# Attention in four passes: the last two products of a pass are held back until the next pass has given out its first scores

## The chip, the cores and the metric

The kernel runs on one core of a Trainium2 chip. The metric is the device time of one execution in microseconds, as a median of several. An execution carries four layers; the change is in the last one.

## The reference, cut to what matters

The input is two images of 128 channels and 64 x 64 places. Four layers follow each other, each adding to its input a result computed from the group-normalized input. Layer 3, with `S` = 4096 places, 8 heads of 16 channels each:

```python
xf = x.reshape(B, C, S)
def proj(wt, bt):
    y = jnp.einsum('oc,bcs->bos', wt, xf) + bt[None, :, None]
    return y.reshape(B, Hh, Dh, S)
q, k, v = proj(wq, bq), proj(wk, bk), proj(wv, bv)
a = jnp.einsum('bhcq,bhck->bhqk', q, k) / jnp.sqrt(jnp.float32(C))
a = jax.nn.softmax(a, axis=-1)
o = jnp.einsum('bhqk,bhck->bhcq', a, v)
return o.reshape(B, C, h, w)
```

and then `x = x + layer3(groupnorm(x))`. So for each image and head there are 4096 x 4096 scores, an exponential of each, and a product with the values.

## The kernel before, in words

Layer 3 (`_layer3`) works in four passes: image 0 with heads 0 to 3, image 0 with heads 4 to 7, and the same for image 1. In a pass four heads lie side by side in the 128 partitions, 32 to each.

Inside a pass, `attend` goes over 8 blocks of 512 queries (`qb`) and in each over 32 tiles of 128 keys (`kt`). Such a step has three parts:

- `scores(qb, kt)`: eight matmuls on TensorE (L2094), two for each of the four heads, into two score tiles in PSUM (`ps_s`; the pool has three such tiles of two banks each). Then ScalarE takes the exponential of each tile (L2104) into two weight tiles in SBUF (`weights`; the pool has eight).
- `multiply(qb, kt, w)`: the product of weights and values (L2113), four matmuls in the source and eight in the profile[...]. They add up over all 32 key tiles in one of two PSUM accumulators (`ps_acc`).
- after the last key tile of a block, `done(qb, ps)`: VectorE copies the accumulator out (L2135), brings the sums to the places of the values (L2137), takes the reciprocal (L2138), multiplies (L2139) and adds the residual (L2140); the result goes out by DMA (L2142).

The order of the instructions on each engine is the order of the program: `_in_order` fixes it. TensorE is therefore kept from waiting for ScalarE by hand: scores are given out two steps ahead of their product. The list `waiting` holds the steps whose product is still to come. After the scores of a step, if more than two steps wait, the product of the oldest is given out. At the end of a pass the two that are left are given out one after the other (L2153 and L2154).

Other work is woven in. `work` is a generator that makes what a pass needs: the folded weights of an image (`folded`), the values (`values`, L2048 and L2055), queries and keys (`queries_and_keys`, L2022 to L2040), and after a pass has begun a bound on its scores (`bound`, L2068 to L2083). While one pass runs, the loop at the end of `_layer3` takes three steps of that generator in each block of queries, so that the next pass finds its queries, keys and values ready. In the first pass part of its own values and keys is made in this way too (`early`).

Of the kernel before, what the change touches and what calls it, by code (L numbers as in the profile page):

```python
# [1954 lines left out]
def _layer3(ctx, tc, X, l3, cst, out, worst, here):  # L1955
# [10 lines left out]
    def acc():  # L1966
        return accp.tile([128, CH], F32, tag="acc", name="ps_acc")
# [118 lines left out]
    def attend(b, t, q, k, vt, early):  # L2086
        ac = [None]

        def scores(qb, kt):
            ps = [spp.tile([128, 2, CH], F32, tag="sp", name="ps_s") for _ in range(2)]  # L2090
            for n in range(2):
                for j in range(4):
                    rows = slice(32 * j, 32 * j + 32)
                    nc.tensor.matmul(  # L2094
                        ps[j // 2][:, j % 2, :],
                        k[rows, kt * 128 : (kt + 1) * 128],
                        q[n][rows, qb * CH : (qb + 1) * CH],
                        start=(n == 0),
                        stop=(n == 1),
                    )  # L2100
            w = []
            for p in range(2):
                w.append(pp.tile([128, 2, CH], F32, tag="weights", name="weights"))
                nc.scalar.activation(w[p], ps[p], AF.Exp)  # L2104
            return w

        def multiply(qb, kt, w):
            if kt == 0:
                ac[0] = acc()
            for j in range(4):  # L2110

                i = j % 2
                nc.tensor.matmul(  # L2113
                    ac[0][32 * j : 32 * j + 32, :],
                    vt[:, kt, j // 2, i : i + 2, :].rearrange("p a d -> p (a d)"),
                    w[j // 2][:, i, :],
                    start=(kt == 0),
                    stop=(kt == NQT - 1),
                )
            if kt == NQT - 1:  # L2120
                done(qb, ac[0])

        def done(qb, ps):
            cols = slice(qb * CH, (qb + 1) * CH)

            places = [
                (slice(32 * j + 16 * (j % 2), 32 * j + 16 * (j % 2) + 16),
                 slice(64 * t + 16 * j, 64 * t + 16 * j + 16))
                for j in range(4)
            ]  # L2130
            xs = residual[qb % 2]
            for to, rows in places:
                nc.sync.dma_start(xs[to, :], X[rows, b, cols])
            u = two.tile([128, CH], F32, tag="u", name="u", bufs=1)
            nc.vector.tensor_copy(u, ps)  # L2135
            r = two.tile([128, CH], F32, tag="r", name="r", bufs=1)
            nc.vector.stream_shuffle(r, u, [(i + 16) % 32 for i in range(32)])  # L2137
            nc.vector.reciprocal(r, r)  # L2138
            nc.vector.tensor_mul(u, u, r)  # L2139
            nc.vector.tensor_add(u, u, xs)  # L2140
            for at, rows in places:
                nc.sync.dma_start(out[b, rows, cols], u[at, :])  # L2142

        waiting = []
        for qb in range(NCH):
            for kt in range(NQT):
                if kt % 2 == 0:
                    over = next(early, early) is early
                waiting.append((qb, kt, scores(qb, kt)))
                if len(waiting) > 2:  # L2150
                    multiply(*waiting.pop(0))
                yield kt if over else None
        for x in waiting:  # L2153
            multiply(*x)  # L2154

    def in_turn(*gens):
        gens = list(gens)
# [7 lines left out]
    def work():  # L2165

        for b in range(B):
            f = []
            yield from folded(b, f)
            for t in range(2):  # L2170
                first = b == 0 and t == 0
                q = [two.tile([128, S], F32R, tag=f"q{n}", name=f"q{n}") for n in range(2)]
                k = two.tile([128, S], F32R, tag="k", name="k")
                vt = two.tile([128, NQT, 2, 3, 16], F32, tag="vt", name="vt")
                early = values(b, t, f, vt)
                keys = queries_and_keys(b, t, f, q, k, 2 * first)
                if first:

                    for _ in range(2):
                        next(keys)  # L2180
                        next(early)
                        yield
                    early = in_turn(keys, early)
                else:
                    for _ in early:
                        yield
                    yield from keys
                yield b, t, (q, k, vt, early)
                yield from bound(b, t, q, k)

    def up_to_next(side):
        for x in side:
            if x:
                found.append(x)
                return
            yield

    side = work()
    found = []
    for _ in up_to_next(side):  # L2200
        pass
    while found:
        b, t, got = found.pop()
        beside = up_to_next(side)
        for kt in attend(b, t, *got):

            if kt in (4, 12, 20):
                next(beside, None)
        for _ in beside:
            pass  # L2210


def _input(nc, X, a, b):
# [31 lines left out]
def kernel(ctx, tc, a, out):  # L2245
# [4 lines left out]
    with tc.tile_pool(name="keep", bufs=1) as keep:  # L2250
# [5 lines left out]
        with tc.tile_pool(name="late", bufs=1) as late:  # L2256
            with tc.tile_pool(name="raw", bufs=1) as raw:
                with tc.tile_pool(name="l1_in", bufs=1) as l1_in:
                    consts = _layer1_inputs(nc, l1_in, a)
                    l3 = _layer3_inputs(nc, late, raw, a, a["consts2"])  # L2260
                    _layer1(tc, X, a, cst, st[:, :B], st[:, B], consts)
                _layer2(
                    tc,
                    X,
                    rows_of_weights,
                    cst,
                    a["consts1"],
                    st[:, B],
                    st[:, B + 1],
                    lambda: _layer3_weights(nc, l3),  # L2270
                )
            _layer3(tc, X, l3, cst, out, worst, st[:, B + 1])
# [69 lines left out]
```

## Time and profile before

| | us |
|---|---|
| executions timed | 4249.1, 4260.06, 4260.55 (median 4260.06) |
| profiled execution | 4252.46, span of the trace 4250.7 |
| TensorE busy (PE) | 4058.6, 95% of the span |
| ScalarE busy (ACT) | 3342.0, 79% |
| VectorE busy (DVE) | 2187.2, 51% |
| DMA, mean | 37 GB/s |
| layer 3 starts at about | 2275 |
| its passes end at about | 2780, 3274, 3764, 4236 |

How to read it: shares are averages over four layers with different limits, so they say little about a single stage. In layer 3 TensorE and ScalarE are both busy in nine tenths or more of nearly every slice, VectorE in one to three tenths. A piece "x8" in a timeline is eight instructions of one kind without a break; the time in front is its start, the next one its length, and what stands in brackets is how long the engine stood idle before it and what ended that. Matmuls overlap, so the lengths of pieces add up to more than the time that passes; the distance between starts doesn't have that fault.

### The profile page before, as it was taken

To read this page: it belongs to the slowest core of one execution; us is meant where nothing else is said; L and a number is where in the kernel's file an instruction comes from. 1 tells how busy PE (TensorE), PEld (TensorE's weight loads), DVE (VectorE), ACT (ScalarE), POOL (GpSimd) and SP (SyncE) were. 2 spreads that over 40 slices of the span, in tenths; PEclk is the share of its full clock that TensorE was granted. 3 is DMA by queue.
4 is the path that set the end of the run, shared out by engine and by line. 5 is a ranking of instruction groups with operands and counts; after the bars stand their busy time and mean duration, and the time that the engine had idled before them with its cause. 6 is when DMAs were issued, how large, how long until landed. Compare 5 with 4: busy or idle time off the path is not lost. (4 is left out here: it accounts for less than half of the span.)

```text
span 4250.7 us, 82260 instructions
## 1 busy us (share of the span) xinstructions
PE 4058.6 (95%) x35790; PEld 1552.1 (37%) x35790; DVE 2187.2 (51%) x2358; ACT 3342.0 (79%) x4051; POOL 70.4 (2%) x145
## 2 busy tenths in 40 slices
PE   7899999978999998997998999999999999999998
PEld 4523222245222223445665333333333333333332
DVE  3679999746999998986765211321032012211111
ACT  4478888734888884335655999999999999999998
POOL 1001000000000001000000000000000000000000
PEclk9999999999999999998999999999999999999999
DMA  1099970000000000003660000000000000000000
GB/s 48 2 194 191 182 89 1 1 1 2 1 1 1 1 1 12 1 1 128 270 263 4 6 6 4 6 6 4 6 6 6 4 6 6 6 4 6 6 6 4
DMA packets 158822, 158.86 MB, mean 37 GB/s; under 512 B 24809, under 2 KB 148713, under 8 KB 154354
## 3 DMA queue, kind: packets, MB, share of 16 engines
q1 hardware_dynamic: 158450, 153.50, 15.5%
q8 instruction: 282, 4.62, 0.4%
q14 instruction: 90, 0.74, 0.1%
HBM read 145.09 MB, written 73.40 MB: 51 GB/s over the span
## 5 line engine op out<-in xcount | busy, mean ns | idle before, releaser
L2104 ACT ACTIVATE weights<-ps_s 128x1024 f32<-128x1024 f32 x2048 | 1885.2, 1103 | 65.9 <-PE ps_s L2094 65.4
L1350 ACT ACTIVATE weights<-ps_s 128x1024 f32<-128x1024 f32 x1024 | 992.6, 1022 | 175.5 <-PE ps_s L1341 150.6
L2113 PE MATMUL ps_acc<-weights,vt 128*32 128x512 f32 x8192 | 1095.6, 607 | 0.0
L2094 PE MATMUL ps_s<-q,k 32*128 32x512 f32 x8192 | 925.9, 445 | 5.3 <-ACT weights L2104 5.3
L1792 DVE TENSOR_TENSOR sums<-sums,weights 128x2048 f32<-128x2048 f32 x384 | 879.1, 2289 | 42.2 <-ACT weights L1350 6.6
L2094 PEld LDWEIGHTS ps_s<-q,k 32*128 32x128 f32 x8192 | 472.6, 183 | 841.9 <-ACT weights L2104 775.2
L1341 PE MATMUL ps_s<-q,k 32*128 32x512 f32 x4096 | 647.4, 642 | 3.7 <-ACT weights L1350 1.3
L2135 DVE COPY u<-ps_acc 128x512 f32<-128x512 f32 x32 | 22.1, 692 | 1041.5 <-PE ps_acc L2113 1041.5
L1757 PE MATMUL ps_acc<-weights,vt 128*32 128x512 f32 x4096 | 548.8, 605 | 3.4 <-ACT used L1782 3.2
L1341 PEld LDWEIGHTS ps_s<-q,k 32*128 32x128 f32 x4096 | 210.4, 183 | 429.7 <-issue 209.9
L2113 PEld LDWEIGHTS ps_acc<-weights,vt 128*32 128x32 f32 x8192 | 163.2, 108 | 378.8 <-issue 366.8
L1757 PEld LDWEIGHTS ps_acc<-weights,vt 128*32 128x32 f32 x4096 | 81.0, 108 | 395.1 <-issue 377.0
L662 DVE SCALAR_TENSOR_TENSOR X<-g,w,X 128x2048 f32<-128x2048 f32 x84 | 197.4, 2351 | 2.6
L1792 DVE TENSOR_TENSOR sums<-weights 128x2048 f32<-128x2048 f32 x64 | 146.6, 2290 | 63.1 <-ACT weights L1350 63.1
L1546 PE MATMUL ps_sp<-pad,diag 32*32 32x512 f32 x4608 | 165.3, 600 | 4.6 <-DVE q L1564 3.1
L1008 PE MATMUL ps_z<-w_ri,e 128*32 128x128 f32 x2048 | 137.5, 409 | 14.4 <-DVE e L950 12.2
L2055 DVE TENSOR_TENSOR vt<-ps_acc,bv 128x384 f32<-128x384 f32 x32 | 17.8, 557 | 247.1 <-PE ps_acc L2048 247.1
L1524 PE MATMUL ps_sp<-xn,w_qkv 128*128 128x512 f32 x160 | 91.3, 709 | 33.5 <-DVE k L1564 16.0
L1546 PEld LDWEIGHTS ps_sp<-pad,diag 32*32 32x32 f32 x4608 | 95.1, 103 | 62.6 <-issue 15.4
L2025 DVE LOAD_MASK_SELECT qq<-ps_acc x32 | 0.4, 14 | 222.2 <-PE ps_acc L2022 222.2
L2138 DVE RECIPROCAL r<-r 128x512 f32<-128x512 f32 x32 | 107.3, 3353 | 1.1
L950 DVE TENSOR_SCALAR e<-ps_pe 32x136 f32<-32x136 f32 (+1 forms) x352 | 104.4, 297 | 5.0
(288 smaller groups left out, 2602.6 us busy)
## 6 DMA issues: line engine op xcount, KB each, us to landing
w_ri<-w_r SPq DMA_DIRECT2D x16, 2112.0 KB, 8.2
w_ri<-w_i SPq DMA_DIRECT2D x16, 2112.0 KB, 13.5
w_r<-in_L_conv_kr_w SPq DMA_DIRECT2D x15, 528.0 KB, 12.5
w_r<-in_L_conv_kr_x SPq DMA_DIRECT2D x15, 528.0 KB, 12.2
w_r<-in_L_conv_kr_y SPq DMA_DIRECT2D x15, 528.0 KB, 12.1
w_r<-in_L_conv_kr_z SPq DMA_DIRECT2D x15, 528.0 KB, 12.4
w_i<-in_L_conv_ki_w SPq DMA_DIRECT2D x15, 528.0 KB, 12.7
w_i<-in_L_conv_ki_x SPq DMA_DIRECT2D x15, 528.0 KB, 12.2
```

The source lines that it names most:

```text
L662: nc.vector.scalar_tensor_tensor(xi, g[:, i : i + H // 2, j : j + W], w8[:, s : s + 1], xi, ALU.mult, ALU.add)
L950: nc.vector.tensor_scalar_mul(out, got[of, :, s], sign)
L1008: nc.tensor.matmul(out.rearrange("p (n f o) -> p n f o", n=2, f=2), e[:, s, 2 * j : 2 * j + 2, :].rearrange("p f x -> p (f x)"), w.rearran ...
L1341: nc.tensor.matmul(ps[j // 2][:, j % 2, :], k[rows, kt * 128 : (kt + 1) * 128], q[rows, qb * CH : (qb + 1) * CH], start=True, stop=True,)
L1350: nc.scalar.activation(w[:, 2 * p : 2 * p + 2, :], ps[p], AF.Exp)
L1546: nc.tensor.matmul(ps[r // 2][to, r % 2, :].rearrange("p (h w) -> p h w", w=W), diag[rows, grp, t, :], pad[rows, y0 : y0 + ROWS, t % 3 : t ...
L1757: nc.tensor.matmul(ac[n][rows, :], lhs(rows), w[:, j, :], start=first, stop=last)
L1792: nc.vector.tensor_add(parts[0].rearrange("p j c -> p (j c)"), t.rearrange("p j c -> p (j c)"), w.rearrange("p j c -> p (j c)"),)
L2094: nc.tensor.matmul(ps[j // 2][:, j % 2, :], k[rows, kt * 128 : (kt + 1) * 128], q[n][rows, qb * CH : (qb + 1) * CH], start=(n == 0), stop= ...
L2104: nc.scalar.activation(w[p], ps[p], AF.Exp)
L2113: nc.tensor.matmul(ac[0][32 * j : 32 * j + 32, :], vt[:, kt, j // 2, i : i + 2, :].rearrange("p a d -> p (a d)"), w[j // 2][:, i, :], star ...
L2138: nc.vector.reciprocal(r, r)
```

## The change: the list of waiting products outlives a pass

Before, `waiting` is made anew in each pass and emptied at its end. After, it is made once in `_layer3`, and what waits is a ready-made call that remembers its pass, its accumulator and its values. A pass ends with two products still waiting; the next pass gives out the scores of its first step, then the product of key tile 30 of the old pass, then its second scores, then the product of tile 31 with the old block's `done`, and from the third scores on its own products. Only after the fourth pass is the list emptied. The purpose is that ScalarE finds scores to work on across the end of a pass, as it does within one.

```diff
-        waiting = []
         for qb in range(NCH):
             for kt in range(NQT):
                 if kt % 2 == 0:
                     over = next(early, early) is early
-                waiting.append((qb, kt, scores(qb, kt)))
+
+                w = scores(qb, kt)
+                waiting.append(lambda qb=qb, kt=kt, w=w: multiply(qb, kt, w))
                 if len(waiting) > 2:
-                    multiply(*waiting.pop(0))
+                    waiting.pop(0)()
                 yield kt if over else None
-        for x in waiting:
-            multiply(*x)
...
     side = work()
-    found = []
+    found, waiting = [], []
     for _ in up_to_next(side):
         pass
...
         for _ in beside:
             pass
+    for x in waiting:
+        x()
```

## The prediction, made before the result was known

> **What bounds the kernel now.** I read the page first: shares by engine, the forty slices, the chain that ended last. All of layer 3 lies in the last 1,970 us (the chain enters its lines at 2275 us).
>
> ```profile
> PE 4058.6 (95%) x35790; PEld 1552.1 (37%) x35790; DVE 2187.2 (51%) x2358; ACT 3342.0 (79%) x4051; POOL 70.4 (2%) x145
> PE ps_acc L2113 24%; PE ps_s L2094 20%; PE ps_acc L2022 1%; PE ps_acc L2048 1%; ACT weights L2104 0%; DVE r L2138 0%; DMA residual<-X 0%; DVE r L2137 0%; DVE u L2139 0%; DVE u L2140 0%; PE ps_acc L2081 0%; DVE u L2135 0%; ACT kk L2031 0%; DVE q L2038 0%; ACT hi L2030 0%
> L2104 ACT ACTIVATE weights<-ps_s 128x1024 f32<-128x1024 f32 x2048 | 1885.2, 1103 | 65.9 <-PE ps_s L2094 65.4
> ```
>
> The end is set by TensorE's two attention lines (24% and 20% of the span). ScalarE's Exp sits just beside them: 2048 of them in 1885 us, idle 65.9 us in all. So in layer 3 there are two full engines, and only time in which both stand can be won. The timeline inside a pass, at the change from one block of 512 queries to the next, shows the steady beat:
>
> ```profile
> 3824.07 1.07 PE L2113 MATMUL ps_acc<-weights,vt 128*32 128x512 f32 x8
> 3825.07 0.91 PE L2094 MATMUL ps_s<-q,k 32*128 32x512 f32 x8
> 3825.90 1.07 PE L2113 MATMUL ps_acc<-weights,vt 128*32 128x512 f32 x8
> 3826.90 0.91 PE L2094 MATMUL ps_s<-q,k 32*128 32x512 f32 x8
> 3827.04 0.69 DVE L2135 COPY u<-ps_acc 128x512 f32<-128x512 f32 x1 [49.38 <-PE ps_acc L2113]
> 3827.74 1.06 PE L2113 MATMUL ps_acc<-weights,vt 128*32 128x512 f32 x8
> ```
>
> One step (scores of a key tile, product of an older one) starts every 1.833 us: 3825.07, 3826.90. The accumulator changes hands at 3827.04 and costs nothing. Exp keeps the same beat: two per step at about 0.91 us from start to start (17 in 15.73 us with the last one's 1.12 us taken off: 14.61 / 16). Now the first end of a pass:
>
> ```profile
> 2776.64 0.91 PE L2094 MATMUL ps_s<-q,k 32*128 32x512 f32 x8
> 2777.48 3.14 PE L2113 MATMUL ps_acc<-weights,vt 128*32 128x512 f32 x24
> 2780.55 0.96 PE L2094 MATMUL ps_s<-q,k 32*128 32x512 f32 x10
> 2781.38 5.76 ACT L2104 ACTIVATE weights<-ps_s 128x1024 f32<-128x1024 f32 x6 [1.87 <-PE ps_s L2094]
> 2782.46 0.73 PE L2094 MATMUL ps_s<-q,k 32*128 32x512 f32 x6 [0.95 <-ACT weights L2104]
> 2785.44 1.94 PE L2113 MATMUL ps_acc<-weights,vt 128*32 128x512 f32 x8
> 2788.46 1.94 PE L2113 MATMUL ps_acc<-weights,vt 128*32 128x512 f32 x8
> 2788.63 1.94 ACT L2104 ACTIVATE weights<-ps_s 128x1024 f32<-128x1024 f32 x2 [1.48 <-PE ps_s L2094]
> 2794.02 0.90 PE L2094 MATMUL ps_s<-q,k 32*128 32x512 f32 x8
> ```
>
> Three products run in one piece (x24, 3.14 us). ScalarE meanwhile finishes the last Exps and stands for 1.87 us. Then TensorE gives out scores with no product between and stands for want of a free score tile (0.95 us, ended by ACT). At last two products take 1.94 us instead of 1.07: the clock fell. The windows give the three ends of passes, the last column but two being the granted clock:
>
> ```profile
> 2770.00:2795.00 25.00, 23.45 (x184) 7.51 (x184) 12.73 (x9) 20.88 (x24) 0.00 (x0) 0.86 0.05 11
> 3265.00:3290.00 25.00, 23.45 (x180) 7.45 (x176) 12.73 (x9) 20.71 (x23) 0.00 (x0) 0.86 0.05 11
> 3755.00:3780.00 25.00, 23.45 (x204) 8.18 (x200) 12.73 (x9) 23.13 (x26) 0.00 (x0) 1.00 0.05 12
> ```
>
> The clock drops to 0.86 at the first two and stays at 1.00 at the third.
>
> [...] TensorE's longest stand here is 0.95 us, with some scattered stops after it. [...] 23.45 of 25 us busy in all three, though the pieces lose quite different times (next part). So I price from start to start.
>
> **The change, part by part.**
>
> *Removed: the drain of the pipeline at three ends.* The end of a pass is measured from the start of its last scores to the start of the seventh scores after it, seven steps on, in steady state 7 x 1.833 = 12.83 us.
> - First: 2794.02 - 2776.64 = 17.38, lost 4.55 us.
> - Second: from the same rows, 3288.75 - 3271.20 = 17.55, lost 4.72 us.
> - Third: 3775.57 - 3760.76 = 14.81, lost 1.98 us.
>
> Sum 11.25 us. ScalarE gives a second price: its idle times there are 1.87 + 1.48 + 0.72, then 1.87 + 1.49 + 0.89, then 1.87: 10.19 us. So the gain in this execution is 10.2 to 11.25, of which 3 x 1.98 = 5.9 is the drain and 5.3 the two clock drops (2.57 and 2.74).
>
> *Added: nothing.* The same 8192 + 8192 matmuls and 2048 Exps run. Only TensorE's order changes: scores 0, product 30, scores 1, product 31 with the old block's `done`, scores 2, product 0. That is the order that already stands between two blocks of one pass, shown at 3827.04 at no cost. So I price the new boundary at zero above the steady 1.833 us.
>
> *New waits.* The first scores now come before products 30 and 31, so a late query or key would hold up both, and `done` behind them. The last piece of the next heads' q is written by VectorE at 2762.00 + 0.75 = 2762.75 us, about 15 us before it would be needed; at the second end 3241.88 + 0.74, over 30 us before. Score tiles: three; weight tiles: eight, of which three steps' worth hold six, as in mid-pass. Both are used as there. `done` starts later than now, after two more scores: about 2776.64 + 0.84 + 1.00 + 2 x 1.83 = 2782.1 instead of 2780.7 us; the five VectorE operations behind it (0.69 + 0.72 + 3.35 + 0.69 + 0.69 = 6.1 us) have one block, about 58 us, to end. Zero on the path.
>
> *Unmoved.* The first pass's beginning and the last end (x24 in 3.1 us, then the reciprocal and the output) stay. So does one other stop with a drop, at 2912 us, where products wait for VectorE's folded weights.
>
> **The time.** The four executions known are 4249.1, 4252.46 (the profiled one), 4260.06 and 4260.55. The middle of the four is (4252.46 + 4260.06) / 2 = 4256.3. The stated median is above it, so I subtract from the middle: 4256.3 - 11.25 = 4245.0, which is 0.35% under 4260.06. From the stated median itself it would be 4248.8, or 0.26%. The gain lies right beside the bound.
>
> **The rivals.**
>
> *A: the drain goes, the drops stay* (or new ones come: [...] other stops remain). Gain 5.9, time 4250. For it: the drop came with stops under 1 us, so little may bring one on. Against: in over 400 us of steady steps in the last pass the granted clock is 1.00 throughout.
>
> *B: ScalarE is the true bound, so filling TensorE only moves a wait.* Time unchanged, 4256. For it: Exp's beat of 0.91 gives 1.83 per step, as long as TensorE's. Against: ScalarE itself idles 1.87 us at each end for lack of scores, and that time it would get back.
>
> *C: slower.* The new heads' scores wait, through a buffer or the fixed order, for the old block's `done`. Then each end costs 6.1 us, the refill of 1.98 and a drop of 2.65: 10.7 instead of the mean 3.75, so 3 x 7 = 21 us more: 4277. Against it: in mid-pass the accumulators are two, and the product after `done` waits only for the copy.
>
> *D: more gain.* In the median run the third end may drop too: 3 x 4.63 = 13.9 us, 4242.4 from the middle.
>
> **How the numbers follow.** The drain and the drops go: 0.74 together with D (D about a quarter of it); A 0.14; B 0.08; C 0.04. The time is that of the likeliest, 4245. Run to run the kernel moves by 11 us, so a median still has some 4 to 5 us either way; 0.3% under 4260.06 is 4247.3, and two thirds of the first case lie below it (0.50), with a quarter of A (0.04): faster 0.54, same 0.42, slower 0.04. The range is from the fastest execution less D, 4249.1 - 13.9 = 4235, to B's 4256.
>
> **What would show it.** In the profile after: at 2776 to 2790 us, and at the two later ends about 5 and 9 us earlier than now, rows of x8 scores and x8 products in turn every 1.83 us, no x24 but the one at the very end; ScalarE's idle before Exp down from 65.9 to about 56 us; granted clock 1.00 in all three windows; the wait of scores on ACT without its 0.95 us pieces. It would be wrong if clock drops turn up elsewhere, if scores of the new heads wait for VectorE, or if the step itself changes from 1.833.

## The result and the profile after

| | before | after |
|---|---|---|
| executions | 6 | 6 |
| median, us | 4258.24 | 4243.2 |
| lowest to highest, us | 4249.1 to 4260.55 | 4239.79 to 4245.4 |
| span of the trace, us | 4250.7 | 4239.7 |

The ratio is 0.9969, with a 95% interval of 0.9956 to 0.9982: 13 us faster, give or take 5.5. The medians lie 15.0 us apart and the two traces 11.0. The prediction's chances of "faster" and "same" part at a gain of 0.3%. By the ratio the gain is 0.31%, with an interval from 0.18% to 0.44%, so on which side of that bound the change lies stays open.

The page after, ScalarE's Exp and TensorE's scores among the groups of instructions (busy time, mean ns of one, then the idle time before them and its releaser):

```profile
L2104 ACT ACTIVATE weights<-ps_s 128x1024 f32<-128x1024 f32 x2048 | 1884.4, 1104 | 55.4 <-PE ps_s L2094 55.0
L2094 PE MATMUL ps_s<-q,k 32*128 32x512 f32 x8192 | 923.4, 443 | 0.7 <-ACT weights L2104 0.7
```

Exp's idle time fell from 65.9 to 55.4 us. TensorE's stops for a score tile, 5.3 us in all before (that group's row in the page of before), are 0.7.

From the timeline after, at the first end of a pass:

```profile
2767.75 33.20 ACT L2104 ACTIVATE weights<-ps_s 128x1024 f32<-128x1024 f32 x36
2777.00 0.91 PE L2094 MATMUL ps_s<-q,k 32*128 32x512 f32 x8
2777.83 1.07 PE L2113 MATMUL ps_acc<-weights,vt 128*32 128x512 f32 x8
2778.83 0.91 PE L2094 MATMUL ps_s<-q,k 32*128 32x512 f32 x8
2779.67 1.07 PE L2113 MATMUL ps_acc<-weights,vt 128*32 128x512 f32 x8
2780.66 0.91 PE L2094 MATMUL ps_s<-q,k 32*128 32x512 f32 x8
2782.63 0.69 DVE L2135 COPY u<-ps_acc 128x512 f32<-128x512 f32 x1 [19.55 <-PE ps_acc L2113]
2783.33 1.07 PE L2113 MATMUL ps_acc<-weights,vt 128*32 128x512 f32 x8
```

The last scores of the old pass start at 2777.00, the new pass's first at 2778.83 and second at 2780.66: the step of 1.83 us doesn't notice the end. Exp runs on through it (36 of them, no break). The copy of the old accumulator stands between two steps as it does in mid-pass. The windows of the three ends, to be held against those of before (the same columns; the clock is the last but two):

```profile
2768.00:2793.00 25.00, 25.00 (x224) 8.62 (x224) 10.22 (x8) 25.00 (x28) 0.00 (x0) 1.00 0.04 10
3260.00:3285.00 25.00, 25.00 (x224) 8.37 (x218) 12.31 (x9) 25.00 (x28) 0.00 (x0) 1.00 0.05 11
3744.00:3769.00 25.00, 25.00 (x224) 8.63 (x216) 11.46 (x9) 25.00 (x28) 0.00 (x0) 1.00 0.05 12
```

TensorE and ScalarE are both busy for the whole 25 us, and the clock is 1.00 at all three.

**A yardstick that single runs can bear.** Layer 3's first accumulator copy starts at 2356.09 us before and 2356.45 after, but over the seven traces here that don't empty the list after the first block it falls anywhere from 2353.02 to 2365.66. Those 12.6 us arise ahead of that copy, and they are more than the two traces differ by. So runs are compared below by the *attention stretch*, from the first start of L2135 to the 32nd: 1880.22 us before, 1868.87 after, 11.35 us less. Where a product list is emptied after the first block already, the first copy comes 1.6 us earlier against its scores (4.03 instead of 5.63 us after the block's last scores). That makes the stretch 1.6 us longer without any loss, so 1.6 us are taken off.

### The profile page after: what moved, and what is told of

Its sections match the earlier page's. It is cut to its first block, busy times and chain, and to the rows that moved or that the text cites. A ratio compares the mean times of both kernels' runs of the same rounds, so it can differ in the third digit from the quotient of the medians.

```text
span 4239.7 us, 82260 instructions
## 1 busy us (share of the span) xinstructions
PE 4053.2 (96%) x35790; PEld 1551.7 (37%) x35790; DVE 2186.7 (52%) x2358; ACT 3341.4 (79%) x4051; POOL 70.6 (2%) x145
## 5 line engine op out<-in xcount | busy, mean ns | idle before, releaser
L2104 ACT ACTIVATE weights<-ps_s 128x1024 f32<-128x1024 f32 x2048 | 1884.4, 1104 | 55.4 <-PE ps_s L2094 55.0
L2135 DVE COPY u<-ps_acc 128x512 f32<-128x512 f32 x32 | 22.1, 692 | 1030.2 <-PE ps_acc L2113 1030.2
```

## The experiments

All are compared with the changed kernel unless it is said otherwise, each by one trace.

**One end drained: the first.** The loop over the passes empties the list once:

```diff
         for _ in beside:
             pass
+        while waiting and (b, t) == (0, 0):
+            waiting.pop(0)()
```

> The changed kernel, but the two waiting products are given out at the end of the first pass alone; the other two ends stay bridged. Theory (each end paid a drain of 1.98 us, and a clock drop of about 2.65 us when one follows): this end costs 4.6 us with a drop in the window or 2.0 without, the other two ends nothing, so the trace's span is 4239.7 + 2.0 to 4.6 = 4241.7 to 4244.3 us. Rival A (the drops don't come from the drain): a drop of the granted clock at this place also in the changed kernel's pattern elsewhere, and no more than 2.0 us. Rival: the three ends don't add up, and one of them alone gives back nearly all 11 us.

The span was 4245.2 us, a little over the range; the first copy had also come 0.4 us later. The attention stretch was 1873.81, that is 4.94 us more. Priced as in the prediction, from the last scores of the pass to the seventh after, this end lost 4.55 us; the other 0.4 us are spread over the stretch. The windows of the three ends:

```profile
2775.00:2800.00 25.00, 23.45 (x184) 7.39 (x176) 12.73 (x9) 20.88 (x23) 0.00 (x0) 0.86 0.05 12
3262.00:3287.00 25.00, 25.00 (x220) 8.46 (x218) 9.02 (x8) 25.00 (x29) 0.00 (x0) 1.00 0.03 7
3748.00:3773.00 25.00, 25.00 (x224) 8.76 (x224) 10.09 (x8) 25.00 (x29) 0.00 (x0) 1.00 0.04 10
```

The drop of the clock comes back at the end that is drained and at no other. The ends add up; each pays for itself.

**One end drained: the third.** The same for another pass:

```diff
+        while waiting and (b, t) == (1, 0):
+            waiting.pop(0)()
```

> The changed kernel, but drained at the end of the third pass alone. Theory: lost at that end 1.98 us if no clock drop follows, 4.6 if one does; the earlier two ends keep the 1.833 us step. Whether the drop comes is chance by the theory (in the kernel before it came at two ends of three); if the place decides instead, it stays away here as it did before, and the loss is 1.98 us.

The attention stretch was 1872.07, 3.20 us more, and the end itself lost 3.23 us: neither number that was expected. The window at that end, TensorE alone (window, its length, busy time and instructions, clock, DMA):

```profile
3750.00:3775.00 25.00, 23.45 (x194) 0.93 0.05 12
```

The clock fell for half as long as at the first end (0.93 against 0.86). So the place doesn't decide: in the kernel before, this end showed 1.00 and lost 1.98. And the drop has more sizes than the two that the prediction reckoned with.

**Half the change: one product held back.**

```diff
         for _ in beside:
             pass
+        while len(waiting) > 1:
+            waiting.pop(0)()
```

> Half the change: at the end of a pass one product is given out and one is held back over the first scores of the next pass. Theory: ScalarE stands for about one product less than the 1.87 us of the full drain, 0.9 us at each end, and TensorE's wait for a free score tile shrinks or goes; so about 1 us lost at each of three ends, 3 us in all, with no clock drop: span about 4243. If a drop needs only a small stop, up to 3 x 3.6 = 11 us. Rival: one product held back hides everything (span 4240), and the second was not needed.

The span, 4238.7 us, seems to speak for the rival. It misleads: the first copy came 3.4 us earlier in this run (at 2353.02). The attention stretch is 1871.58, which is 2.71 us more than with two. From scores to scores the three ends lost 0.76, 0.75 and 0.76 us, 2.27 in all. The timeline at the first of them shows where:

```profile
2773.65 0.91 PE L2094 MATMUL ps_s<-q,k 32*128 32x512 f32 x8
2774.49 1.92 PE L2113 MATMUL ps_acc<-weights,vt 128*32 128x512 f32 x16
2776.34 0.96 PE L2094 MATMUL ps_s<-q,k 32*128 32x512 f32 x10
2777.17 18.44 ACT L2104 ACTIVATE weights<-ps_s 128x1024 f32<-128x1024 f32 x20 [0.65 <-PE ps_s L2094]
2778.25 0.73 PE L2094 MATMUL ps_s<-q,k 32*128 32x512 f32 x6 [0.95 <-ACT weights L2104]
```

Two products in one piece, 1.92 us, leave ScalarE without scores for 0.65 us instead of 1.87. TensorE still stands 0.95 us for a free score tile, against what was expected, but no clock drop follows at any of the three ends; at the first (TensorE alone):

```profile
2774.00:2799.00 25.00, 24.05 (x216) 1.00 0.05 12
```

So one product held back brings back most of it, and the second is worth 2.3 us over the three ends, or 2.7 by the stretch.

**A drain after every block.** The list is emptied at the end of each of the 32 blocks of queries:

```diff
                 yield kt if over else None
+            while waiting:
+                waiting.pop(0)()
```

> The changed kernel, but the list is emptied after each of the 8 query blocks of every pass: 32 drains, 31 of them more than in the changed kernel (the last end has one in all). Theory: 31 drains at 1.98 us without and 4.63 us with a clock drop; with drops after two of three as before, 31 x 3.75 = 116 us: about 4243 + 116 = 4359; bounds 61 us (no drop) and 144 us (a drop at each). Rival (the drain itself is free and only the passes' ends are special, through new queries, keys and values): the blocks inside a pass cost nothing more than the three ends, 11 us.

Executions took 4349.41 and 4335.3 us, ratio to the kernel before 1.0211 (1.0156 to 1.0265). The attention stretch was 1970.91: less 1868.87 and the 1.6 us of the yardstick that makes 100.4 us for 31 drains, 3.24 each. The 16 us from the three products on, for three of the drains (TensorE alone):

```profile
2419.80:2435.80 16.00, 14.50 (x106) 0.79 0.08 17
3834.41:3850.41 16.00, 14.46 (x126) 1.00 0.08 17
4019.02:4035.02 16.00, 14.46 (x114) 0.89 0.08 17
```

Of the 31 drains 12 kept 1.00, 13 fell to 0.79 and 6 to 0.89. Drains without side work in reach lost 1.98 us at 1.00 (at 3834 us), 3.25 at 0.89 (at 4019 us) and 4.50 at 0.79 (at 2420 us). So a block in mid-pass pays the same as an end of a pass, and the rival, that the ends are special, is out. The mean came out under the 3.75 expected, mainly because a third of the drops were half drops.

Narrower windows show what a full and a half drop are:

```profile
2426.02:2432.85 6.83, 6.46 (x36) 0.50 0.10 24
3330.55:3333.96 3.41, 3.41 (x22) 0.50 0.06 15
```

The clock in these drops was 0.50; the 13 full ones lasted 6.83 us each, the 6 half ones 3.41. The starts of all 19 lie whole multiples of 3.413 us apart (the first two, 2426.02 and 2490.87, are 64.85 = 19 x 3.413 apart). In the trace before, the drops at the first two ends of passes, 6.83 us at 0.50 each, have the same spacing: they start at 2783.79 and 3278.72, and 494.93 / 145 is 3.413. Points 3.413 us apart, counted on from the drops of a run, are called its ticks below. Where a tick fell after the copy of the drained accumulator sorts all 31 drains: at 2.93 to 3.54 us a full drop began there, at 3.69 to 4.72 a half one, and where no tick fell from 2.93 to 4.72 there was none. The five drained ends shown so far (three in the kernel before, one in each of the first two experiments) fit: their drops began 3.12, 3.50, 3.14 and 4.27 us after the copy, and the end without one had its ticks outside. So in these 36 drains what had been taken for chance was the place of the drain between two ticks. Nor was one product held back merely lucky: counted from the start of its 0.95 us stop, the ticks fell at 3.03, 3.62 and 2.63 us, and after the same stop of the full drains drops began at 2.08 to 3.87.

**What brings the drop: filling TensorE's stops.** First on the kernel before, three ends, with a small filling:

```diff
                 waiting.append((qb, kt, scores(qb, kt)))
+                if qb == 0 and kt < 2 and (b, t) != (0, 0):
+                    fill = acc()
+                    for n in range(2 - kt):
+                        nc.tensor.matmul(
+                            fill, k[:32, :128], q[0][:32, :CH], start=True, stop=True
+                        )
```

> The kernel before, drains and all, but at the three ends TensorE gets idle work: two matmuls of 32 x 128 by 32 x 512 into an accumulator that nobody reads after the first scores of the new pass, and one after the second scores, where it otherwise stands for want of a score tile. Theory (drain and clock drop are two costs, and the drop comes from TensorE's stops): the drain's 1.98 us stay at each end, or become up to 2.8 where the filling overlaps the return of a tile, and the drops at the first two ends go: span 4250.7 - 5.3 = 4245.4, up to 4248. Rival: the drops stay with TensorE filled, [...] since the stops don't cause them: 4250.7 or more.

The windows of its three ends:

```profile
2787.00:2812.00 25.00, 23.92 (x207) 8.24 (x203) 12.73 (x9) 23.13 (x26) 0.00 (x0) 1.00 0.05 12
3277.00:3302.00 25.00, 23.92 (x185) 7.93 (x181) 12.73 (x9) 20.75 (x24) 0.00 (x0) 0.86 0.05 12
3767.00:3792.00 25.00, 23.92 (x211) 8.36 (x209) 12.73 (x9) 23.13 (x26) 0.00 (x0) 1.00 0.05 11
```

One drop of three, where the kernel before had two: this decides nothing, since two of the ends had no tick where a drop had followed a drain. The span, 4256.4, says nothing either, since the first copy came 9.6 us later (at 2365.66). The attention stretch is 1876.54, 3.68 less than before, but 1.3 of that is the stop near 2910 us, which came without its drop in this run.

Then with a drain after every block, where 31 drains give a count, and two, two and one such matmuls after the first three scores of a block:

```diff
+                if kt < 3 and qb + t + b > 0:
+                    fill = acc()
+                    for n in range(2 - kt // 2):
+                        nc.tensor.matmul(
+                            fill, k[:32, :128], q[0][:32, :CH], start=True, stop=True
+                        )
```

> The kernel drained after every block, with idle work for TensorE after each drain but those at the start of the first pass: two matmuls of 32 x 128 by 32 x 512 into an unread accumulator after the first scores, two after the second and one after the third. Drained without filling, 19 of 31 drains were followed by a clock drop (13 at 0.79 and 6 at 0.89 in the 16 us from the three products on) and a drain cost 3.2 us in the mean. Theory (TensorE's stops after the drain bring the drop): with them filled, 6 drops or fewer, and about 2 us, up to 2.8 with the overlap of filling, for each drain: attention from the first to the last accumulator copy about 1870 + 31 x 2.0 to 2.8 = 1932 to 1957 us. Rival (the stops aren't the cause[...]): 15 drops or more, and 1971 us or more.

Drops followed 17 of 31 drains (7 at 0.79, 10 at 0.89), and the attention stretch was 1962.18: less 1868.87 and 1.6, 91.7 us or 2.96 a drain. Both are misses for the theory. By the ticks, 18 of these drains lay where an unfilled drain always had a drop, 9 of them where it was a full one; 16 of the 18 had one, 7 of them full; the 17th drop began 3.61 us after the copy, between the two stretches. So this filling took away next to nothing.

Last, the same with filling of the products' own kind, 128*32 by 128x512 where the small filling has 32*128 by 32x512:

```diff
+                if kt < 2 and qb + t + b > 0:
+                    fill = acc()
+                    for j in range(4):
+                        nc.tensor.matmul(
+                            fill[32 * j : 32 * j + 32, :],
+                            vt[:, 0, j // 2, j % 2 : j % 2 + 2, :].rearrange("p a d -> p (a d)"),
+                            X[:, b, :CH],
+                            start=True,
+                            stop=True,
+                        )
```

> The kernel drained after every block, with idle work of the products' own kind after each drain but those at the start of the first pass: four matmuls of 128 x 32 by 128 x 512 (a product of the values and the input[...]) into an unread accumulator after the first and again after the second scores. Theory (it is TensorE's activity after the drain that counts, [...]): 6 drops or fewer of 31, and 2 to 3 us for a drain: 1932 to 1963 us from the first to the last accumulator copy. Rival (the drops aren't set by the stops after the drain): 15 drops or more as in the two runs before, 1965 us or more.

```profile
2348.69:2364.69 16.00, 16.00 (x142) 1.00 0.08 18
2409.33:2425.33 16.00, 16.00 (x142) 1.00 0.08 17
3853.42:3869.42 16.00, 16.00 (x142) 1.00 0.08 18
```

No drop at all: over the 31 drains from 2352 to 4243 us, windows of 61 us without a gap show 1.00 throughout. It wasn't luck of the ticks: this trace has drops ahead of the drains (at 2279.03) and behind them (at 4286.07), 588 x 3.413 apart, and by their ticks 14 of the 31 drains lay where an unfilled drain always had a drop. The attention stretch is 1929.43, which leaves 1929.43 - 1868.87 - 1.6 = 59.0 us, 1.90 a drain: the drain alone (1.98 at 1.00 without filling), so the filling took no time that wasn't lost already. The kernel does more work than the one with empty stops and its stretch is 41.5 us shorter. This is what parts the two costs: 1.9 us of drained pipeline that this filling didn't give back, and a clock drop that went with what TensorE did after the drain (after 19 of 31 drains without filling, after none of 31 with this one). The small filling, matmuls of 32 rows in part of the stops (TensorE still stood 0.48 and 0.41 us after a drain), was not enough: 17 of 31.

**Beyond the change: the stop that it left.** The woven-in work is taken later in a block:

```diff
-            if kt in (4, 12, 20):
+            if kt in (8, 16, 24):
```

> The changed kernel, with the woven-in work taken at key tiles 8, 16 and 24 of a block instead of 4, 12 and 20, so that the folded weights of image 1 no longer queue on VectorE behind the old block's reciprocal. Theory: the stop that the change left at about 2908 us (3.7 us lost against the step of 1.833, TensorE waiting for VectorE's folded weights) shrinks to about 1 us with no clock drop: 2 to 3 us less than the changed kernel, span about 4237, ratio to the kernel before about 0.9963. Rival: the stop is in the dependence of those few operations themselves and stays: 4239.7.

Nine executions had a median of 4240.0 us (4235.4 to 4249.04); the ratio to the kernel before is 0.9969 (0.9959 to 0.998), the same as the change alone, so the whole time can't tell the two apart. The attention stretch can: 1866.64 us, 2.23 less. The timeline around the old stop:

```profile
2908.63 0.35 DVE L1988 TENSOR_SCALAR wqk<-w_qk,gn_got 128x256 f32<-128x256 f32 x1
2914.09 1.06 PE L2113 MATMUL ps_acc<-weights,vt 128*32 128x512 f32 x8
2915.08 0.61 PE L1997 MATMUL ps_acc<-gn_got,wqk 128*128 128x1 f32 x4
2915.94 0.59 PE L2005 MATMUL ps_acc<-wv,means 128*128 128x192 f32 x2 [0.25 <-DVE both L1999]
```

VectorE now has the folded weights ready 6 us before TensorE asks, so the first product (L1997) no longer stands. In the changed kernel it stood 1.21 us, with a drop after it:

```profile
2908.11 0.61 PE L1997 MATMUL ps_acc<-gn_got,wqk 128*128 128x1 f32 x4 [1.21 <-DVE wqk L1988]
```

Only the 0.25 us for VectorE's difference (L1999) is left. Only this trace shows it as the better of the two, and part of the 2.23 us may be luck: from its last scores to those of the next, the block with that stop takes 64.36 us in the changed kernel and 61.88 here, but 63.15 in the run with the three filled ends, where the stop stood as before and no drop followed.

## Why the prediction was right

- *The drain is removed whole.* Right. The price was 11.25 us; the attention stretch fell by 11.35, of which 0.1 belongs to the stop near 2910 us, whose block took 64.36 instead of 64.47 us. It was the price of one execution with two full drops: by the mean of the drained blocks, 3.24, three ends would cost an estimated 9.7 us.
- *Added: nothing.* Right. The new boundary keeps the step of 1.83, and the product behind `done` waits for the copy alone, as in mid-pass: at the first end it starts at 2783.33, where the copy ends (2782.63 + 0.69).
- *New waits: none.* Right: the copy of the old accumulator came 5.63 us after the last scores (5.5 expected), and the five VectorE operations behind it held up nobody.
- *5.9 us of drain and 5.3 of clock drops.* Right in kind, shown by the filled drains (1.90 each with no drop) and by the drained blocks. The size of a drop was too simple: besides full drops of 2.5 to 2.7 us there are half drops of 1.3.
- *ScalarE's idle time as the second price.* Right: 10.19 us by its pieces, 10.5 by its row in the page. That is against rival B, in which a ScalarE bound leaves the time as it was.
- *Rival A*, drops that stay: the clock was 1.00 at all three ends, and between the first block and the last end the trace has one drop, the one near 2910 us that was there before. *Rival C*, slower through a wait for `done`: no such wait. *Rival D*, a drop at the third end too in the usual run before: possible, since the ratio gives 13 us where the traces give 11, but the interval takes in both, so it stays open. By the ticks it is a matter of where that end falls: its clock was 1.00 before and 0.93 in the run that drained it alone.
- *The time.* 4243.2 for 4245.0, and so close partly by luck. The base, the middle of the four executions known, was 4256.3, which is 1.9 below the median of the six (4258.24). The gain taken off was 11.25, which is 3.8 less than the 15.0 between the medians. The two misses pull against each other.

## What to carry to other kernels

Where scores are given out ahead of their products by a hand-written list, let the list outlive the loop that fills it. Both engines are full here, and every emptying between two blocks cost time (1.9 to 2.0 us for two products, 0.76 where only one was given out), and many a clock drop on top (1.3 or 2.5 to 2.7 us). To price such an end, measure from start to start against the steady step, and split off the drop by comparing like ends. When runs differ by more than the effect, compare a stretch inside the trace that begins after the noise.

## What the runs showed of the hardware that was not expected

- The granted clock fell after stops of TensorE of 0.95 us or less each, after 19 of 31 like drains: to 0.50, for 3.41 or 6.83 us, with starts whole multiples of 3.413 us apart. In the 36 drains without filling, whether and how long went by where a tick fell after the copy: a full drop at 2.93 to 3.54 us, a half one at 3.69 to 4.72, none elsewhere.
- The longest stop didn't decide it: with one product held back, the same 0.95 us brought no drop at three ends. In the run drained after every block, TensorE's stops in the 3.41 us before a tick added up to 1.08 us or more where a drop began, and to 0.95 or less where the clock stayed at 1.00. This is no rule for every case: near 2919 us in the run with filled ends 1.10 us brought no drop, and with the small filling after every block 0.55 us was enough.
- What filled the stops mattered. Matmuls of 32*128 by 32x512 left drops after 17 of 31 drains; matmuls of 128*32 by 128x512, in longer pieces (1.07 us against 0.62), left none. Whether the rows or the share of time filled made the difference was not tried apart.
- Added work on TensorE made the drained kernel faster, by 41.5 us in the attention stretch.
